# First attention of a two-layer transformer: the value products in two halves between the score rounds, and one of two shifts made by ScalarE and GpSimd

## The chip, the cores and the metric

The kernel runs on one core of a Trainium2 chip. A core has TensorE (matrix products, written PE in the profile, its weight loads PEld), VectorE (DVE), ScalarE (ACT), GpSimd (POOL) and SyncE (SP, which issues most DMAs here). Each engine works through its own instructions in order, and waits for the others by semaphores. Products land in PSUM, which has eight banks of 128 partitions by 512 numbers. The metric is the time of one execution on the device in microseconds (us); smaller is better.

## The reference

The reference takes 64 sequences of 128 tokens with 128 features, all in float32, and applies two layers. Each layer is an attention with 16 heads of 8 features and then a mixture of 8 experts of which 2 are chosen for each token; each part is added to its input, and each starts from a layer norm.

```python
x = x + _L0_xattn_ref(_layernorm(x, axis=-1), fside_BxSxS_0, ctx_1024, ctx_1024, ...)
x = x + _L0_ffn_ref(_layernorm(x, axis=-1), L0_ffn_wqkv, L0_ffn_w1, L0_ffn_w2)
x = x + _L1_xattn_ref(_layernorm(x, axis=-1), ctx_1024, ctx_1024, ...)
x = x + _L1_ffn_ref(_layernorm(x, axis=-1), ...)
```

The first attention is what this case is about. For each sequence, queries come from x. Keys and values come from 128 rows of a side input that are projected, and from 120 rows of a context that are used as they are, so there are 248 keys. Then

```python
attn = jnp.einsum('bhqd,bhkd->bhqk', q, k) * scale
attn = jax.nn.softmax(attn, axis=-1)
out = jnp.einsum('bhqk,bhkd->bhqd', attn, v)
return out.transpose(0, 2, 1, 3).reshape(Bn, Nq, C) @ Wp + bp
```

## The kernel before

The 64 sequences are handled one by one ("batches" in the code), in 16 groups of four (`GB = 4`). `attention` is a pipeline over iterations `it`, one for each batch and five more. In iteration `it` the kernel works on several batches at once:

- **Maxima of batch `it`.** The scores with queries as rows (`max_bank`, L394) are made only for their largest value in each row, which VectorE takes (L414, negated, into `nm`).
- **Shift of batch `it - 1`.** TensorE turns `nm` (two transposes at L459), and VectorE adds the turned maxima to the stored queries `q4` in places where a head's spare feature is multiplied by a one among the keys (L462, once for each half `v` of the heads). So the scores of the second kind come out with the maximum already subtracted.
- **Scores of batch `it - 2`.** They are made again with keys as rows (`score_bank`, L430), and ScalarE takes the exponential into `p` (L438).
- **Values of batch `it - 3`.** `values` (L475) multiplies `p` with the values, which carry a column of ones that gives the sum of each row. There are two halves `v`, with 16 matmuls each, that fill two halves of one bank. ScalarE copies the bank to `ov` (L484, `out1`). TensorE turns it (L491, `out2`), VectorE takes reciprocals of the sums (L495) and scales (L497).
- **Output of batches `it - 4` and `it - 5`.** `out3` turns the result (L504) and ScalarE copies it (L506); `out4` multiplies with the output weights (L511), and `out5` adds to x (L516), followed by statistics for the norms (L109).

The scores are made in four rounds. Each round fills four banks, two with scores for maxima and two with scores for exponentials: TensorE issues the first matmuls of all four, then the second ones, and after that come two maxima on VectorE and two exponentials on ScalarE. All products of the stage draw their bank from one pool of eight (`mtile`); a new one takes the bank that was given back first.

The order is written out by hand: within this stage each engine executes its instructions in the order in which the code emits them. In the first attention an iteration reads:

```python
rounds(0, 1)
on(5, out4); on(1, shift); on(5, out5)
aside.ahead(it); aside.call(it, mtile)
on(3, *vals)
...
prep(it, 0); aside.call(it, mtile)
rounds(2, 3)
on(4, out3); on(3, out2); prep(it, 1)
```

`prep` makes the next group ready, a piece in each half of an iteration. With j the iteration's number modulo 4: at j = 0 the queries (`prep_q`, L292, one matmul and four activations at L301, two in each half, all from one bank); at j = 2 the values of the side input (`prep_v`, L214 and two VectorE additions at L221) in the first half and the keys (`prep_k`, L202 and two activations at L207) in the second; at j = 3 the transposes of x (`prep_x`, L176 and a copy at L177). `context` loads the context's keys (L261) and values (L266) for the next group at j = 2. GpSimd makes the normed x (L167) and its bias (L526).

`aside.call`, twice in an iteration, runs a piece of the first expert layer's router for groups that are done: transposes and logits (L176, L681), choices of the experts by many small VectorE operations, counting (L831), and two indirect DMAs in most iterations, which GpSimd issues (L807). `aside.end` issues zero writes from SP (L1278) that wait for an iteration's L495. After the first attention come the experts' tiles, the second attention (which uses the same function with `first` false), and the second experts.

Of the kernel before, what the change touches and what calls it, by code (L numbers as in the profile page):

```python
# [8 lines left out]
F32 = mybir.dt.float32  # L9
I32 = mybir.dt.int32  # L10
AF = mybir.ActivationFunctionType
ALU = mybir.AluOpType
# [6 lines left out]
GB = 4  # L19
# [25 lines left out]
def transformer_kernel(ctx, tc, a, out):  # L45
# [186 lines left out]
    def attention(layer, w, norm, first, aside):  # L232
# [5 lines left out]
        with ExitStack() as es:  # L238
# [78 lines left out]
            def prep_v(g):  # L317
                values_of(w, src[g], g, n0, mtile())
# [20 lines left out]
            def prep(it, half):  # L339

                g, j = it // GB + 1, it % GB
                if not first:
                    if g == 1:
                        if (j, half) == (0, 0):
                            prep_k(1)
                            prep_v(1)
                        elif (j, half) == (0, 1):
                            prep_x(1)
                        elif j == 1:
                            prep_q(1, half)  # L350
                            if half:
                                prep_heads(1)
                    elif g < NG:
                        pieces = (
                            (), (lambda: prep_k(g), lambda: prep_heads(g)),
                            (lambda: prep_v(g), lambda: prep_x(g)),
                            (lambda: prep_q(g, 0), lambda: prep_q(g, 1)),
                        )[j]
                        if half < len(pieces):
                            pieces[half]()  # L360
                    return
                if half == 0 and it < GB - 1:
                    prep_batch(it + 1)
                if (it, half) == (0, 1):
                    prep_v(0)
                    norm_of(1)
                if (it, half) == (1, 1):
                    biased(0)
                if (it, half) == (2, 1):
                    prep_x(1)  # L370
                if (it, half) == (3, 0):
                    prep_q(1, 0)
                    prep_q(1, 1)
                if (j, half) == (3, 1):
                    if g + 1 < NG:
                        prep_x(g + 1)
                elif g >= NG:
                    return
                elif j == 0 and it:
                    prep_q(g, half)  # L380
                elif (j, half) == (2, 0):
                    prep_v(g)
                elif (j, half) == (2, 1):
                    prep_k(g)


# [68 lines left out]
            def shift(b):  # L455
                g, j = divmod(b, GB)
                pm = mtile()[:, : 2 * S]
                for i in range(2):
                    nc.tensor.transpose(pm[:, i * S : (i + 1) * S], nm[b % 2][:, i, :], ident)  # L459
                for v in range(NV):  # L460
                    q = q4s[g][:, j, 2 * v : 2 * v + 2, :].rearrange("p i q -> p (i q)")
                    nc.vector.scalar_tensor_tensor(  # L462
                        q, pm, smask[:, v : v + 1], q, ALU.mult, ALU.add
                    )

            def values(b, v):
                g, j = divmod(b, GB)
                if v == 0:
                    pavs[b] = mtile()
                pav = pavs[b]  # L470
                p = ps_[b]
                for i in range(2):
                    for c, (_, n) in enumerate(chunks):
                        for ra in range(4):
                            nc.tensor.matmul(  # L475
                                pav[32 * ra : 32 * ra + 32, v * S : (v + 1) * S],
                                lhsT=vs[g % 2][c][:, j, 4 * v + ra, i, :],
                                rhs=p[:n, c, ra, (2 * v + i) * S : (2 * v + i + 1) * S],
                                start=(i == 0 and c == 0), stop=(i == 1 and c == nc_ - 1),
                            )  # L480

            def out1(b):
                ov = rows.tile([128, NV * S], F32, name="ov", tag="ov")
                nc.scalar.copy(ov, pavs.pop(b)[:, : NV * S])  # L484
                ots[b] = ov

            def out2(b):
                ov = ots.pop(b)
# [64 lines left out]
            for it in range(B + 5):  # L553
                def on(back, *steps):
                    b = it - back
                    if 0 <= b < B:
                        for f in steps:
                            f(b)
# [16 lines left out]
                if first:  # L575
# [5 lines left out]
                    on(5, out5)  # L581
                    aside.ahead(it)
                    aside.call(it, mtile)
                    on(3, *vals)
                    if it % GB == 2 and it // GB + 1 < NG:
                        context(it // GB + 1)
                    prep(it, 0)
                    aside.call(it, mtile)
                    rounds(2, 3)
                    on(4, out3)  # L590
                    on(3, out2)
                    prep(it, 1)
                    aside.end(it, work, mtile)
                else:
                    on(3, *vals)
# [970 lines left out]
```

## Time and profile before

| what | us |
|---|---|
| median of three runs | 1524.06 |
| lowest and highest of them | 1517.69, 1524.3 |
| the profiled execution | 1516.1 |
| its span, first to last instruction | 1514.3 |
| TensorE matmuls busy, in the span | 1421.0 |
| VectorE busy | 1102.4 |
| ScalarE busy | 847.6 |
| GpSimd busy | 640.4 |
| maxima, L414, 768 of both attentions | 463.5 |
| shifts, L462, 256 of both attentions | 111.1 |
| copies of the value products, L484, 128 | 48.1 |

The profile is of one execution. A row of a group gives the line, the engine, the operation, what is written and read, its shape and its count; then the busy time and the mean of one in nanoseconds; then the idle time of the engine just before it and who ended most of it. A row of the timeline gives the start, the time, the engine, the line and the operation, with a count where equal ones were merged, and in brackets an idle time before it. A row of the windows gives, for one stretch, the busy time of PE, PEld, DVE, ACT and POOL with their counts, the granted clock, the DMA share and GB/s. Ends of matmuls are modelled and they overlap, so that the busy share of PE is no measure of how near it is to its peak. In float32 each matmul has two records.

### The profile page before, as it was taken

The numbers are of one execution on the slowest core, as the hardware profiler recorded it, in microseconds if no ns is written. First come the engines' busy times: TensorE is split into PE (matmuls) and PEld (weight loads), VectorE is DVE, ScalarE is ACT, GpSimd is POOL, SyncE is SP. The second block draws the span as 40 slices with busy tenths as digits, with TensorE's granted clock in tenths as the row PEclk, the third lists the DMA queues.
The fourth block names the chain that finished last, engine by engine and source line by source line (L and its number), as shares of the span: only waits on it lengthen the run. The fifth ranks groups of instructions, "written<-read, shape, count | busy, mean of one in ns | idle before, by whom it ended". The sixth has DMA issues, their size and how long they took to land.

```text
span 1514.3 us, 42033 instructions
## 1 busy us (share of the span) xinstructions
PE 1421.0 (94%) x16620; PEld 1107.5 (73%) x16620; DVE 1102.4 (73%) x3024; ACT 847.6 (56%) x1740; POOL 640.4 (42%) x1195
## 2 busy tenths in 40 slices
PE   7999999999999999888999999898999999999987
PEld 5777777777777677777888888566666776767665
DVE  6777888888888988455754444687777778787763
ACT  4666666666666666543333333566667566666643
POOL 4123254646465635654001122377546555454210
PEclk9999999999999999999999999899999999999999
DMA  8433333333222221366766667111011111100000
GB/s 201 120 80 80 79 82 96 89 93 94 63 66 60 58 73 40 107 184 202 214 197 199 201 195 205 49 34 34 22 36 29 39 35 32 31 29 23 8 16 22
DMA packets 143719, 133.03 MB, mean 88 GB/s; under 512 B 48546, under 2 KB 126114, under 8 KB 141602
## 3 DMA queue, kind: packets, MB, share of 16 engines
q1 hardware_dynamic: 135330, 113.02, 27.3%
q0 software_dynamic: 8192, 17.32, 3.7%
q8 instruction: 132, 2.16, 0.6%
q14 instruction: 65, 0.53, 0.1%
HBM read 97.32 MB, written 32.97 MB: 86 GB/s over the span
## 4 chain that ended last, share of the span: by engine, by line
PE 69%; DVE 15%; DMA 4%; POOL 4%; ACT 4%; issue 2%; SPq 1%; POOLq 0%; DVEq 0%; ACTq 0%
PE bank L430 11%; PE bank L394 10%; PE bank L475 9%; PE bank L1115 9%; PE bank L1424 4%; PE bank L1445 4%; DVE nm L414 4%; PE bank L1128 3%; DMA q<-xs 2%; PE bank L407 2%; PE bank L214 2%; DVE q L462 2%; PE bank L511 2%; PE bank L681 2%; PE bank L202 2%
## 5 line engine op out<-in xcount | busy, mean ns | idle before, releaser
L414 DVE TENSOR_REDUCE nm<-bank 128x2 f32<-128x496 f32 (+1 forms) x768 | 463.5, 662 | 77.6 <-PE bank L430 61.8
L438 ACT ACTIVATE p<-bank 120x512 f32<-120x512 f32 (+1 forms) x768 | 402.1, 605 | 126.8 <-PE bank L430 123.9
L430 PE MATMUL bank<-q,k 32*120 32x256 f32 (+1 forms) x3072 | 438.1, 399 | 11.4 <-DVE nm L414 5.2
L430 PEld LDWEIGHTS bank<-q,k 32*120 32x120 f32 (+1 forms) x3072 | 293.5, 181 | 56.8 <-DVE nm L414 17.3
L394 PE MATMUL bank<-k,q 32*128 32x248 f32 x2048 | 291.0, 399 | 0.7 <-ACT q L334 0.5
L394 PEld LDWEIGHTS bank<-k,q 32*128 32x128 f32 x2048 | 202.2, 189 | 47.9 <-issue 11.0
L1120 DVE TENSOR_TENSOR p<-p,bank 128x256 f32<-128x256 f32 x213 | 88.0, 420 | 121.0 <-ACT p L1119 120.5
L475 PE MATMUL bank<-p,v 128*32 128x128 f32 (+1 forms) x4096 | 175.6, 275 | 0.2
L407 PE MATMUL bank<-k,qf 32*128 32x480 f32 x512 | 153.8, 602 | 0.8 <-ACT qf L295 0.8
L807 POOL DMA_INDIRECT xs<-xn,at x128 | 129.2, 1009 | 27.9 <-issue 24.3
L1119 ACT ACTIVATE p<-bank 128x256 f32<-128x256 f32 x213 | 81.0, 384 | 98.9 <-PE bank L1115 97.9
L484 ACT COPY ov<-bank 128x256 f32<-128x256 f32 x128 | 48.1, 376 | 143.5 <-PE bank L475 143.4
L475 PEld LDWEIGHTS bank<-p,v 128*32 128x32 f32 (+1 forms) x4096 | 108.8, 109 | 22.8 <-issue 13.7
L1364 POOL DMA_INDIRECT yb<-ys,back x112 | 108.5, 969 | 27.7 <-issue 19.5
L1115 PE MATMUL bank<-q 128*128 128x256 f32 x516 | 118.6, 379 | 1.6 <-ACT q L1106 1.6
L462 DVE SCALAR_TENSOR_TENSOR q<-bank,c_smask,q 128x256 f32<-128x256 f32 x256 | 111.1, 475 | 8.2 <-PE bank L459 7.8
L167 POOL TENSOR_SCALAR xn<-x,mv,rstd 128x128 f32<-128x128 f32 x252 | 110.2, 449 | 7.5 <-issue 1.4
L1115 PEld LDWEIGHTS bank<-q 128*128 128x128 f32 x516 | 94.7, 190 | 13.0 <-ACT q L1106 1.9
L475 PE MATMUL bank<-p,vc 120*32 120x128 f32 x2048 | 103.2, 272 | 0.0
L155 POOL TENSOR_SCALAR rstd<-mv 128x4 f32<-128x4 f32 x32 | 6.3, 198 | 219.9 <-DVE mv L113 123.0
L301 ACT ACTIVATE q<-bank,c_a_bq,c_hmask 128x512 f32<-128x512 f32 x124 | 90.1, 789 | 9.8 <-PE bank L292 9.8
L1157 POOL DMA_INDIRECT kvT<-ys,back x16 | 15.4, 961 | 189.7 <-DMA vc<-xs 114.0
(224 smaller groups left out, 2465.7 us busy)
## 6 DMA issues: line engine op xcount, KB each, us to landing
q<-in_w SPq DMA_DIRECT2D x43, 576.0 KB
vc<-in_w SPq DMA_DIRECT2D x28, 576.0 KB
vc<-in_ctx_v SPq DMA_DIRECT2D x16, 960.0 KB
ys<-zero SPq DMA_DIRECT2D x71, 128.0 KB
k<-in_ctx_k SPq DMA_DIRECT2D x32, 240.0 KB
q<-xs SPq DMA_DIRECT2D x43, 128.0 KB
ys<-q SPq DMA_DIRECT2D x43, 128.0 KB
x<-in_x SPq DMA_DIRECT2D x16, 256.0 KB
```

What stands on the lines that cost most here:

```text
L167: nc.gpsimd.tensor_scalar(xn[:, j, :D], xg[g][:, j, :], self.mv[:, b, 0:1], self.rstd[:, b : b + 1], ALU.add, ALU.mult,)
L301: nc.scalar.activation(q4s[g][:, :, s, :], pq.rearrange("p (b q) -> p b q", b=GB), AF.Identity, bias=w["bq"][:, s : s + 1], scale=hmask[:, ...
L394: nc.tensor.matmul(pa[:, u, :], lhsT=q4s[g][r, j, s, :], rhs=k2[g % 2][r, s // 2, j, :], start=True, stop=True,)
L407: lambda: nc.tensor.matmul(pa, lhsT=qfs[g][r, j, :], rhs=k4s[g][r, :, j, :], start=True, stop=True),
L414: nc.vector.tensor_reduce(nm[b % 2].rearrange("q i (a s) -> q a i s", s=16)[:, 2 * ra + v : 2 * ra + v + len(slots) // 2, :, 0], pa.rearra ...
L430: nc.tensor.matmul(pb[:n, v * 256 : (v + 1) * 256], lhsT=k2[g % 2][r, v, j, k0 : k0 + n], rhs=q4s[g][r, j, 2 * v : 2 * v + 2, :].rearrange ...
L438: nc.scalar.activation(ps_[b][:n, c, ra, :], pb[:n], AF.Exp, scale=SCALE)
L462: nc.vector.scalar_tensor_tensor(q, pm, smask[:, v : v + 1], q, ALU.mult, ALU.add)
L475: nc.tensor.matmul(pav[32 * ra : 32 * ra + 32, v * S : (v + 1) * S], lhsT=vs[g % 2][c][:, j, 4 * v + ra, i, :], rhs=p[:n, c, ra, (2 * v + ...
L807: s = nc.gpsimd.indirect_dma_start(xs, bass.IndirectOffsetOnAxis(at[:, j, k : k + 1], 0), xn, None)
L1115: nc.tensor.matmul(ph[:, u, :], lhsT=w[:, c, u * 128 : (u + 1) * 128], rhs=xT, start=True, stop=True)
L1364: nc.gpsimd.indirect_dma_start(y[:, k, b % 2, :], None, ys, bass.IndirectOffsetOnAxis(back[:, b, k : k + 1], 0),)
```

## The change

The change touches the first attention alone.

- Values are made in two halves that have a bank each. `half_out(b, 0)` stands where all of the values stood, ahead of rounds 2 and 3; `half_out(b, 1)` stands behind them. After each half ScalarE copies 128 columns to `ov`, where one copy of 256 columns was made before.
- Of the two shifts of a batch the second (`v` = 1) is no longer made by VectorE. ScalarE copies the turned maxima, scaled by the mask, to a tile `sh` (which shares its two buffers with `ov`), and GpSimd adds `sh` to the queries.
- `prep_v` for the next group moves behind rounds 2 and 3 of the same iteration, with `context`, and `prep_k` takes its place ahead of them.
- `out2` moves behind `prep(it, 1)`.

```diff
@@ prep @@
                 elif (j, half) == (2, 0):
-                    prep_v(g)
-                elif (j, half) == (2, 1):
                     prep_k(g)
@@ shift @@
                 for v in range(NV):
                     q = q4s[g][:, j, 2 * v : 2 * v + 2, :].rearrange("p i q -> p (i q)")
+                    if first and v:
+
+                        sh = rows.tile([128, 2 * S], F32, name="sh", tag="ov")
+                        nc.scalar.activation(sh, pm, AF.Copy, scale=smask[:, v : v + 1])
+                        nc.gpsimd.tensor_tensor(q, q, sh, ALU.add)
+                        continue
                     nc.vector.scalar_tensor_tensor(
                         q, pm, smask[:, v : v + 1], q, ALU.mult, ALU.add
                     )
@@ values @@
-                if v == 0:
+                if v == 0 or first:
                     pavs[b] = mtile()
@@ after out1 @@
+            def half_out(b, v):
+
+                values(b, v)
+                if v == 0:
+                    ots[b] = rows.tile([128, NV * S], F32, name="ov", tag="ov")
+                cols = slice(v * S, (v + 1) * S)
+                nc.scalar.copy(ots[b][:, cols], pavs.pop(b)[:, cols])
@@ the loop over iterations, first attention @@
                     aside.call(it, mtile)
-                    on(3, *vals)
-                    if it % GB == 2 and it // GB + 1 < NG:
-                        context(it // GB + 1)
+                    on(3, lambda b: half_out(b, 0))
                     prep(it, 0)
                     aside.call(it, mtile)
                     rounds(2, 3)
+                    on(3, lambda b: half_out(b, 1))
+                    if it % GB == 2 and it // GB + 1 < NG:
+                        context(it // GB + 1)
+                        prep_v(it // GB + 1)
                     on(4, out3)
+                    prep(it, 1)
                     on(3, out2)
-                    prep(it, 1)
                     aside.end(it, work, mtile)
```

## The prediction

> **What bounds the kernel now.** I read the page's engine row first, then the windows, then the timeline of each engine over four iterations, because the change lies in the first attention alone (about 15 to 625 us).
>
> ```profile
> PE 1421.0 (94%) x16620; PEld 1107.5 (73%) x16620; DVE 1102.4 (73%) x3024; ACT 847.6 (56%) x1740; POOL 640.4 (42%) x1195
> L484 ACT COPY ov<-bank 128x256 f32<-128x256 f32 x128 | 48.1, 376 | 143.5 <-PE bank L475 143.4
> L462 DVE SCALAR_TENSOR_TENSOR q<-bank,c_smask,q 128x256 f32<-128x256 f32 x256 | 111.1, 475 | 8.2 <-PE bank L459 7.8
> ```
>
> ```profile
> 200.00:400.00 200.00, 197.39 (x3037) 149.63 (x3033) 171.22 (x432) 129.61 (x262) 116.10 (x259) 1.00 0.32 85
> ```
>
> In that window (columns PE, PEld, DVE, ACT, POOL, clock, DMA) TensorE looks full and VectorE is 86% busy. But matmuls overlap, so the share hides stalls. The pace shows them: with every bank free, a pair of rounds (32 matmul records) takes 1.91 us to issue. That is what the second rounds from 323.69 to 325.60 take; from 316.76 to 319.71 the first rounds take 2.95:
>
> ```profile
> 315.23 0.47 PE L430 MATMUL bank<-q,k 32*120 32x256 f32 x1 [0.31 <-DVE nm L414]
> ...
> 316.28 0.33 PE L504 MATMUL bank<-ident,o 128*128 128x128 f32 x1
> ...
> 318.66 0.48 PE L430 MATMUL bank<-q,k 32*128 32x256 f32 x1
> ...
> 319.71 0.49 PE L511 MATMUL bank<-c_a_wo,oT 128*128 128x128 f32 x2
> ```
>
> ```profile
> 317.13 1.47 ACT L301 ACTIVATE q<-bank,c_a_bq,c_hmask 128x512 f32<-128x512 f32 x2
> ```
>
> At 315.23 and 318.66 TensorE resumes when a PSUM bank comes back: the first from VectorE's maximum, the second from ScalarE's query activations. So the bound is TensorE plus the return of eight banks. Iterations begin at 316.76, 326.14, 336.04, 345.08, 354.46, 363.85, 373.97, 382.26 and 391.65: 74.89 us for eight, 9.36 each. Call them phases 1, 2, 3, 0, 1', 2', 3', 0' (iteration number modulo 4; the router's work differs between the two groups). Over 1.91 us, the first rounds lose 1.04, 0.86, 0.75, 0.5 in phases 1, 2, 3, 0; the second rounds lose 1.0 in phase 0 alone, where the query bank leaves only seven. The reason is visible: 1.90 us of values plus output work stand ahead of the second rounds, but only 0.54 us of transposes ahead of the first.
>
> **The change, part by part**, in us from the first matmul of an iteration. From the timelines: the first maximum starts 1.13 after its round pair, four take 2.34; the first exponential 1.18, four take 1.92; out4 with the shift's transposes is 0.63 of TensorE; values 1.90, so a half 0.95; a bank is used again 0.07 after its reader; a second round needs its last bank at +0.90, and lasts 1.05 from there.
>
> *Removed from VectorE:* one of two shifts, 0.39 back to back, so 64 x 0.39 = 25 us of busy time. It shortens the time from the first rounds' last maximum (3.47) to the router's operations.
>
> *Added to ScalarE:* the scaled copy of 128x256, which no row shows. Nearest is the copy-out of that size, 0.376; the 128x512 query activation with scale and bias is 0.79. Bounds 0.37 to 0.79; I take 0.40. Two copies of 128x128 replace one of 128x256: 2 x 0.29 (the row of oT's copy) - 0.376 = +0.2. ScalarE goes from 6.0 to 6.6 us of 9.4, so its busy time isn't the price; its order is.
>
> Here a rule speaks against the change. The Trainium skill, "PSUM — Partial Sum Buffer", section on bank collisions: two engines may not touch the same bank and quadrant at once, reads against reads included. The shift's bank now has two readers, and in the built program the scaled copy indeed waits for VectorE's shift. Without the rule it would run at 3.10, when the exponentials end; with it at 3.47 + 0.39 + 0.07 = 3.93, done at 4.33. Queued behind it are half 0's copy-out, then phase 1's xnT copy, phase 3's router exponential, phases 0 and 2's query or key activations, and the second rounds' exponentials. In phases 0 and 2 nothing is lost (query or key matmul ends at 4.55 anyway). In phase 1 the logits matmul waits for xnT: 4.33 + 0.60 + 0.07 = 5.00 against 4.69, +0.31. In 3' half 0's copy-out ends at 5.22, and the last bank of the second rounds is 0.88 late.
>
> *Added to GpSimd:* an add of 128x256; its row, `x<-x,yb` of the same size, has 0.734. Its result is due at the next iteration's first score matmuls, some 5 us after 4.33, so it is hidden; were the cover gone it would cost 0.73 x 64 = 47 us. Behind it wait the router's operations and indirect DMAs; only phase 2' feels it: products 1.07 on GpSimd, for which a VectorE reduction waits until 6.27 (the maxima behind it slip 1.3). A second rule, "SBUF — State Buffer", section "SBUF: two separate sides": a GpSimd operation that reads SBUF and a VectorE one with two SBUF inputs exclude each other for the whole instruction. The rows don't agree:
>
> ```profile
> 322.32 0.22 DVE L719 TENSOR_TENSOR eq<-eq,order 128x64 f32<-128x64 f32 x1
> ```
>
> ```profile
> 322.25 0.21 POOL L138 TENSOR_TENSOR mv<-st 128x4 f32<-128x4 f32 x1 [2.49 <-DVE st L109]
> 322.41 0.20 POOL L139 TENSOR_TENSOR d<-st 128x4 f32<-128x4 f32 x1
> ```
>
> VectorE's product of two SBUF tiles runs through both in its usual 0.22. I take nothing; by the rule up to 0.73 an iteration, 47 us.
>
> *Moved on TensorE:* half of the values, 0.95, from ahead of the second rounds to behind them. Gains: the first rounds find their banks free (1.91 in phases 0, 2, 3). Losses: the second rounds start 0.95 earlier relative to VectorE's work; and out2 now needs the second half's copy-out. That wait is new: half 1 ends at E, its copy runs E + 0.13 to E + 0.40 (or behind the exponentials), the second transpose at 0.07 more, the next rounds 0.2 later: 0.67 after E, where out3 and out2 took 0.48. Behind it stand all next rounds. Value projection (1.09, phase 2) and xnT's transposes (0.56, phase 3) fill it.
>
> *Moved with it:* prep_k's matmul (1.06) and two activations (1.34) from behind the second rounds to ahead of them in phase 2, prep_v the other way with its two VectorE adds (0.67 back to back). SP's values DMA of the context waits for half 1 instead; behind it stand only zero writes and the next load, and it is needed five iterations later: nothing. Its two key DMAs don't wait for the values: nothing.
>
> **The sum.** Phase 1: query activations of phase 0 still hold a bank until 1.53; first rounds end 2.58; out4, shift, xn transposes (0.53) to 3.74, half 0 to 4.69, logits 5.00 to 6.00, second rounds to 7.91, half 1 to 8.86, exponentials end 9.10, copy 9.37, next rounds 9.64 (was 9.38).
> Phase 2: 1.91 + 0.63 + 0.95 + 1.06 = 4.55; the last bank waits for the key activations (4.65 + 1.53), rounds end 7.23, half 1, prep_v, out3, out2: 9.75 (was 9.90).
> Phase 3: the router's counting matmul waits for its VectorE operand, which was 5.02 into the iteration and is now ready at 4.77; TensorE now comes at 3.51, waits to 4.94: 9.40 (was 9.04).
> Phase 0: second rounds start at 4.55, their last bank needs the first new maximum, VectorE is at the router until 5.95: bank at 6.60, rounds end 7.65; 9.27 (was 9.38).
> By the same steps 1' 9.64 (9.39), 2' 10.12 (10.12), 3' 8.33 (8.29), 0' 9.54 (9.39).
> Together 75.69 against 74.89: +0.8 for eight, x 8 = +6.4 us. The profiled execution took 1516.1 (span 1514.3 and 1.8 around it), so it would take 1522.5; the median shown is 1524.06, 8 above it, and the forecast stands on that: 1530. In short, the removed stalls (about 2.5 us per four iterations) come back as later banks in the second rounds, a logits wait, a counting wait and the copy-out.
>
> **Rivals.** *The stalls really go (1494):* the first rounds' stalls fall by 0.5, 0.5, 0.86, 0.7 in phases 0 to 3, and neither the second rounds nor out2 take it back; less 0.19 x 2 of longer tails that is about 2.2 per four, or 35 us over 64. For it: VectorE's 86%, relieved by 0.39 an iteration. Against it: VectorE works 2.1 to 2.8 us between the two round pairs even so, and TensorE then arrives 0.95 earlier. Chance 0.22.
> *ScalarE's queue becomes the chain (1556, slower):* the place is the scaled copy behind VectorE's shift. My sum has 0.3 us or less to spare between it and the query and key activations. If the first rounds' maxima end later than about 3.5, or the copy takes the upper bound's 0.79, each further 0.1 moves activations, exponentials and half 1's copy by 0.1; at 0.4 that is 64 x 0.4 = 26 us more. For it: the ordering is certain. Against it: VectorE's maxima ended 3.47 to 3.8 after the start already. Chance 0.31.
> *Nothing moves:* DMA and GpSimd hide all; it falls in the likeliest case.
>
> **Numbers.** The likeliest case, 1530 with its own range 1518 to 1544 (0.1 to 0.2 us an iteration of error in the steps), has 0.47: 0.03 of it faster, 0.22 the same, 0.22 slower. The rivals give 0.20 faster and 0.02 same, and 0.29 slower and 0.02 same. A difference under 0.5% (7.6 us; the three runs spread 0.43%) can't be told from none. Faster 0.23, same 0.26, slower 0.51. The range takes in both rivals' values and a little of the added bounds: 1498 to 1562.
>
> **What would show it.** First rounds near 1.91 us in phases 0, 2, 3; the scaled copy starting right behind VectorE's shift; TensorE's wait ahead of out2's second transpose in phases 0 and 1; the counting matmul waiting for VectorE; the second rounds of phase 2 near 2.7; the add done 3 us or more before its reader. An iteration under 9.0 us on average, or over 9.7, makes the forecast wrong.

## The result, and the profile after

The changed kernel took 1535.65 us (median of seven executions), the kernel before 1521.57 on the same chip: a ratio of 1.0092, with a 95% interval of 1.0074 to 1.011, or 14 us more. One of the seven took 6383 us and is left out of the ratio. The profiled execution took 1536.61, its span 1534.8 (before: 1516.1 and 1514.3).

The page's engine row, and from it and the list of all groups the rows of the lines that were changed (busy us, mean ns of one, then the idle time before it):

```profile
PE 1413.3 (92%) x16620; PEld 1094.3 (71%) x16620; DVE 1092.1 (71%) x2960; ACT 880.0 (57%) x1868; POOL 688.7 (45%) x1259
L466 DVE SCALAR_TENSOR_TENSOR q<-bank,c_smask,q 128x256 f32<-128x256 f32 x192 | 86.0, 475 | 8.7 <-PE bank L457 8.5
L464 POOL TENSOR_TENSOR q<-q,sh 128x256 f32<-128x256 f32 x64 | 47.9, 749 | 253.7 <-ACT sh L463 240.7 <-DVE eq L732 7.8 <-DVE te_i_a L948 5.1
L497 ACT COPY ov<-bank 128x128 f32<-128x128 f32 x128 | 34.4, 269 | 20.4 <-PE bank L479 20.4
L463 ACT ACTIVATE sh<-bank,c_smask 128x256 f32<-128x256 f32 x64 | 30.4, 475 | 56.4 <-DVE q L466 56.4
```

GpSimd is 48.3 us busier, ScalarE 32.4. VectorE loses only 10.3, although its shifts' row fell by 25.1 (111.1 to 86.0): other operations of it got longer, above all a 128x64 product (5.3 us over 38), a 128x8 operation with a scalar (2.7 over 19), a scan (2.6 over 8) and a cast (1.0 over 16). The last row's idle time, 56.4 us, is the scaled copy waiting for VectorE's shift of the same bank. The window between 200 and 400 us (PE, PEld, DVE, ACT, POOL, clock, DMA share, GB/s):

```profile
200.00:400.00 200.00, 189.10 (x2979) 141.25 (x2983) 164.90 (x400) 138.67 (x301) 127.47 (x268) 1.00 0.32 85
```

TensorE's busy time in it fell from 197.39 to 189.10 at an unchanged clock: it waits more. Where it waits is read from TensorE's timeline, cut into four stretches for each phase: first rounds, what stands between ("middle"), second rounds, and what stands behind them up to the next iteration ("tail"). Here are the stretches between 240 and 480 us, where the pattern of eight iterations repeats within 0.03 us:

| phase | before: first, middle, second, tail | period | after: first, middle, second, tail | period | forecast |
|---|---|---|---|---|---|
| 1 | 2.96, 3.97, 1.91, 0.54 | 9.38 | 2.38, 3.67, 1.99, 1.73 | 9.77 | 9.64 |
| 2 | 2.77, 3.62, 2.03, 1.48 | 9.90 | 1.91, 2.71, 2.66, 2.43 | 9.71 | 9.75 |
| 3 | 2.66, 3.28, 1.91, 1.19 | 9.04 | 2.20, 3.29, 1.91, 1.93 | 9.33 | 9.40 |
| 0 | 2.41, 3.59, 2.92, 0.48 | 9.39 | 1.93, 2.71, 3.38, 1.73 | 9.75 | 9.27 |
| 1' | 2.96, 3.98, 1.91, 0.54 | 9.39 | 2.38, 3.67, 1.91, 1.81 | 9.76 | 9.64 |
| 2' | 2.77, 3.62, 2.09, 1.64 | 10.12 | 1.91, 2.71, 3.08, 2.43 | 10.14 | 10.12 |
| 3' | 2.66, 2.53, 1.91, 1.19 | 8.29 | 2.20, 1.65, 2.54, 1.93 | 8.32 | 8.33 |
| 0' | 2.40, 3.59, 2.92, 0.48 | 9.39 | 1.91, 2.71, 3.34, 1.73 | 9.69 | 9.54 |

Eight iterations take 76.49 us instead of 74.89. That is +1.6, or 12.8 us if all 64 iterations were like these. They are not quite: over the 58 full iterations of the two traces (539.2 and 552.5 us) the difference is 13.3 us. The first eight are 1.6 faster, each of the next four eights is 1.6 slower, and the eight from 437 us on are 4.2 slower. There one phase 0 takes 13.31 us instead of 9.75 (10.28 in the kernel before), with TensorE's granted clock (third number from the right) at a half:

```profile
512.00:519.00 7.00, 6.58 (x64) 4.71 (x67) 2.75 (x6) 3.08 (x6) 4.26 (x9) 0.51 0.06 20
```

In the kernel before, the clock is 1.00 in these 7 us. Whether the change brings the half clock about is not shown.

The tail contains half 1 of the values (0.95) now, and the middle lacks it. So the first rounds are shorter everywhere, as the removed stalls said; the second rounds are longer in both phases 2 and 0 and in 3', and the tail is longer by more than half 1 in both phases 0 and 1 (0.48 to 1.73, 0.54 to 1.73 or 1.81).

The wait that sets phase 0, and the scaled copy, in the timelines of TensorE and ScalarE after (phase 0 begins at 350.88):

```profile
357.85 0.47 PE L428 MATMUL bank<-q,k 32*120 32x256 f32 x1 [0.77 <-DVE nm L412]
```

```profile
354.92 0.47 ACT L463 ACTIVATE sh<-bank,c_smask 128x256 f32<-128x256 f32 x1 [0.80 <-DVE q L466]
355.29 0.26 ACT L497 COPY ov<-bank 128x128 f32<-128x128 f32 x1
...
360.05 0.27 ACT L497 COPY ov<-bank 128x128 f32<-128x128 f32 x1 [0.33 <-PE bank L479]
```

TensorE's last bank of the second rounds comes 6.97 after the phase began, from VectorE's maximum; 6.60 was forecast. Why VectorE is late is in its own timeline. First VectorE in two places, then GpSimd in the same two:

```profile
336.65 0.63 DVE L733 TENSOR_TENSOR eq<-eq,order 128x64 f32<-128x64 f32 x1
...
355.69 0.70 DVE L856 TENSOR_TENSOR_SCAN sums<-flat,zero 128x64 f32<-128x64 f32 x1
```

```profile
336.43 0.78 POOL L464 TENSOR_TENSOR q<-q,sh 128x256 f32<-128x256 f32 x1 [0.32 <-ACT sh L463]
...
355.48 0.76 POOL L464 TENSOR_TENSOR q<-q,sh 128x256 f32<-128x256 f32 x1 [4.33 <-ACT sh L463]
```

The product of two SBUF tiles is the operation that the prediction showed at 0.22 beside small GpSimd operations; beside the 128x256 add it takes 0.63. The scan takes 0.70, and 0.29 in the kernel before:

```profile
350.43 0.29 DVE L842 TENSOR_TENSOR_SCAN sums<-flat,zero 128x64 f32<-128x64 f32 x1
```

Both end just after the add does (337.28 against 337.21, 356.39 against 356.24).

### The profile page after: what moved, and what is told of

Read it like the earlier page. It is cut to its first block, busy times and chain, and to the rows that moved or that the text cites. A ratio compares the mean times of both kernels' runs of the same rounds, so it can differ in the third digit from the quotient of the medians.

```text
span 1534.8 us, 42093 instructions
## 1 busy us (share of the span) xinstructions
PE 1413.3 (92%) x16620; PEld 1094.3 (71%) x16620; DVE 1092.1 (71%) x2960; ACT 880.0 (57%) x1868; POOL 688.7 (45%) x1259
## 3 DMA queue, kind: packets, MB, share of 16 engines
q8 instruction: 131, 2.15, 0.6%
## 4 chain that ended last, share of the span: by engine, by line
PE 58%; DVE 22%; ACT 7%; POOL 5%; DMA 5%; issue 3%; SPq 0%; POOLq 0%; ACTq 0%; DVEq 0%
PE bank L1129 9%; DVE nm L412 8%; PE bank L428 7%; PE bank L479 7%; PE bank L392 7%; PE bank L1438 4%; PE bank L1459 4%; PE bank L1142 3%; ACT p L436 3%; DVE q L466 3%; DMA q<-xs 2%; PE bank L405 2%; PE bank L214 2%; DMA vc<-xs 2%; PE bank L503 2%
## 5 line engine op out<-in xcount | busy, mean ns | idle before, releaser
L428 PE MATMUL bank<-q,k 32*120 32x256 f32 (+1 forms) x3072 | 419.6, 396 | 17.3 <-DVE nm L412 10.6
L392 PE MATMUL bank<-k,q 32*128 32x248 f32 x2048 | 268.2, 397 | 0.5 <-ACT q L334 0.5
L392 PEld LDWEIGHTS bank<-k,q 32*128 32x128 f32 x2048 | 189.8, 191 | 39.0 <-DVE st L109 15.2
L479 PE MATMUL bank<-p,v 128*32 128x128 f32 (+1 forms) x4096 | 179.2, 280 | 6.5 <-DVE nm L412 5.6
L464 POOL TENSOR_TENSOR q<-q,sh 128x256 f32<-128x256 f32 x64 | 47.9, 749 | 253.7 <-ACT sh L463 240.7
L479 PEld LDWEIGHTS bank<-p,v 128*32 128x32 f32 (+1 forms) x4096 | 104.9, 110 | 51.8 <-DVE nm L412 27.2
L167 POOL TENSOR_SCALAR xn<-x,mv,rstd 128x128 f32<-128x128 f32 x252 | 111.1, 453 | 8.6 <-issue 2.5
L466 DVE SCALAR_TENSOR_TENSOR q<-bank,c_smask,q 128x256 f32<-128x256 f32 x192 | 86.0, 475 | 8.7 <-PE bank L457 8.5
```

The costliest lines, as they stand in the source:

```text
L167: nc.gpsimd.tensor_scalar(xn[:, j, :D], xg[g][:, j, :], self.mv[:, b, 0:1], self.rstd[:, b : b + 1], ALU.add, ALU.mult,)
L392: nc.tensor.matmul(pa[:, u, :], lhsT=q4s[g][r, j, s, :], rhs=k2[g % 2][r, s // 2, j, :], start=True, stop=True,)
L428: nc.tensor.matmul(pb[:n, v * 256 : (v + 1) * 256], lhsT=k2[g % 2][r, v, j, k0 : k0 + n], rhs=q4s[g][r, j, 2 * v : 2 * v + 2, :].rearrange ...
L466: nc.vector.scalar_tensor_tensor(q, pm, smask[:, v : v + 1], q, ALU.mult, ALU.add)
L479: nc.tensor.matmul(pav[32 * ra : 32 * ra + 32, v * S : (v + 1) * S], lhsT=vs[g % 2][c][:, j, 4 * v + ra, i, :], rhs=p[:n, c, ra, (2 * v + ...
```

## The experiments

The experiments ran on other chips than the measurement above, and a kernel's time differs between these by up to 3.6% (the kernel before: 1518 to 1573 us), so each is set against the kernel before on its own chip, by the ratio. Part of what the chips do differently turned out to matter here: how much an indirect DMA of the router disturbs the engines around it.

A second measure goes round that. Iterations 13 to 20 (the eight that end at about 200 us) come before the first indirect DMA, and there the changed kernel takes the same time on the three chips on which it was profiled: 76.47 us on the first, 76.48 and 76.47 on two others. So the traces of all versions can be compared there. A later eight (29 to 36, from about 280 us) shows what the time with the indirect DMAs adds. Each value is from one execution:

| version | iterations 13 to 20 | against the kernel before, times 8 | iterations 29 to 36 |
|---|---|---|---|
| kernel before, first chip | 74.89 | | 74.90 |
| changed kernel, first chip | 76.47 | +12.6 | 76.48 |
| changed kernel again | 76.48 | +12.7 | 81.93 |
| split alone | 76.07 | +9.4 | 78.45 |
| shift alone | 74.75 | -1.1 | 75.88 |
| scaled copy first | 74.99 | +0.8 | 78.59 |
| add twice | 77.50 | +20.9 | 81.62 |
| without the add | 75.60 | +5.7 | 82.44 |
| output's transposes later | 75.81 | +7.4 | 79.52 |
| router's second piece later | 72.88 | -16.1 | 76.29 |
| that, and the add later | 72.04 | -22.8 | 86.01 |

The sections below call the first column the undisturbed iterations. It leaves out what the router does only later: the router's second piece moved, without indirect DMAs, takes 72.90 in the first column and 73.23 in the last.

### The split alone, and the shift alone

The split alone keeps both shifts on VectorE:

```diff
 for v in range(NV):
     q = ...
-    if first and v:
-        sh = rows.tile(...)
-        nc.scalar.activation(sh, pm, AF.Copy, scale=smask[:, v : v + 1])
-        nc.gpsimd.tensor_tensor(q, q, sh, ALU.add)
-        continue
     nc.vector.scalar_tensor_tensor(...)
```

> Both shifts on VectorE again, the rest of the change kept. Theory (the moved half of the values costs, because VectorE's work between the round pairs loses its cover): nearly the whole slowdown stays, 1530 to 1540 against 1521 before, since VectorE gets 0.39 us per iteration more while ScalarE's wait for it is gone. Rival (the hand-over of the shift to ScalarE and GpSimd costs): most of the 14 us is gone, 1521 to 1527.

The shift alone puts these five lines into the kernel before, with all values in one piece ahead of the second rounds.

> The kernel before with the second shift by ScalarE and GpSimd alone. Theory: 1.9 us of value products cover both the 0.39 us that VectorE saves and the later scaled copy, so nothing moves, 1516 to 1526. Rival (the hand-over costs): 1529 to 1535. If VectorE's busy time were the bound: 64 x 0.39 = 25 us less, about 1497.

Measured: the split alone 1.0094 (1.0062 to 1.0126), the shift alone 1.0005 (0.9986 to 1.0024). VectorE's relief and the new hand-over over ScalarE and GpSimd, taken alone, change nothing that can be measured; in the kernel before, both have cover. That holds for GpSimd's add too: with the shift alone it lengthens the same VectorE operations as in the changed kernel (the eight scans take 4.9 us together, 2.35 in the kernel before), and it costs nothing. The split alone makes the kernel slower, by some 15 us on this chip. The whole change costs 35 us there (below), so the split and the shift do not simply add up: in the split kernel the shift by ScalarE and GpSimd costs about 20 us more. In the undisturbed iterations it is only 0.4 us in eight, 3 us in all. Most of the rest goes with the indirect DMAs: with the split alone 22 copies start late for 22 us in all, in the changed kernel 26 for 33 us. In the profile of the split alone the logits' wait of phase 1 is shorter than in the changed kernel (middle 3.09, not 3.67), since no scaled copy stands ahead of the xnT copy, and the second rounds take most of it back (2.44, not 1.99). In phase 0', with both shifts on VectorE, TensorE waits 1.07 us for VectorE's maximum:

```profile
315.59 0.47 PE L428 MATMUL bank<-q,k 32*120 32x256 f32 x1 [1.07 <-DVE nm L412]
```

### The scaled copy ahead of VectorE's shift

```diff
-for v in range(NV):
+for v in ((1, 0) if first else (0, 1)):
```

> The changed kernel with the order of the two shifts turned: ScalarE's scaled copy first, so it doesn't wait for VectorE's shift on the same bank. Theory: the copy starts about 0.8 us earlier, which gives back about 0.3 us in phase 1 (the logits wait for xnT) and 0.4 in every second phase 3, and GpSimd's add ends before VectorE's router operations start, which gives back about 0.4 in phase 0: 8 to 14 us less than the changed kernel, about 1524. Rival (the order on the bank is not on the path): within 3 us of 1535.

Measured 1.0084 (1.0058 to 1.0109). The changed kernel itself on that chip, run later, gave 1.0228 (below), so this order is some 22 us better there, more than expected. Part of that is the indirect DMAs again (18 late copies of 17 us, not 26 of 33). In the undisturbed iterations it is 1.5 us in eight, or 12 us over 64, which is what was expected. The scaled copy now runs as soon as the exponentials are done, and what stood behind it comes earlier: in 2' the products on GpSimd (second rounds 2.66, not 3.09), in 1' the logits (middle 3.09, not 3.67), in 3' half 0's copy (second rounds 2.21, not 2.54), in 0 VectorE's router (3.18, not 3.39). VectorE's shift is later for it, and some comes back: phase 1's middle is 3.09 (3.67) but its second rounds are 2.33 (1.99), in phase 3 the counting matmul makes the middle 3.47 (3.29), and in 0' the second rounds are 3.46 (3.34).

### GpSimd's add twice

```diff
 nc.gpsimd.tensor_tensor(q, q, sh, ALU.add)
+again = rows.tile([128, 2 * S], F32, name="again", tag="again", bufs=1)
+nc.gpsimd.tensor_tensor(again, sh, sh, ALU.add)
```

> The changed kernel with a second GpSimd addition of the same size behind the first (sh + sh into a tile that nobody reads). Theory (GpSimd's add and VectorE's operations between SBUF tiles exclude each other, as the 0.70 us scan and the 0.69 us tensor_scalar in the changed kernel's trace suggest): up to 0.75 us more of VectorE's router time where it is on the path, 8 to 20 us slower than the changed kernel, and again VectorE operations that last until the end of an addition. Rival (the two engines don't hinder each other): 0 to 3 us slower.

Measured 1.027 (1.0238 to 1.0302). Against the changed kernel's 1.0228 (1.0199 to 1.0257) on that chip this is about 7 us, with intervals that overlap. The undisturbed iterations show it more surely: 1.0 us more in eight, or 8 us over 64, with 0.58 of it in phase 2' (10.73 against 10.14, where the products wait behind both adds) and 0.30 in phase 0 (10.05 against 9.75). The second add is 39.7 us of GpSimd's time, so most of it is hidden. The scan of phase 0 takes 702 ns here, no more than with one add: it is the first add that meets it. The second add meets the operation behind the scan, a 128x8 one of two SBUF tiles that takes 0.17 otherwise. It ends with the add, and TensorE's wait for the first new maximum grows from 0.77 to 1.07:

```profile
284.14 0.42 DVE L864 TENSOR_TENSOR start<-filled,sums 128x8 f32<-128x8 f32 x1
```

```profile
283.92 0.61 POOL L466 TENSOR_TENSOR again<-sh 128x256 f32<-128x256 f32 x1
```

### The changed kernel again, and without the add

The changed kernel as it is:

> The changed kernel itself, on the chip that the following kernels use, so that each can be set against it. If the price of the change belongs to the program and not to one chip, the ratio to the kernel before is again 1.007 to 1.011, and the stretches of each phase come out as in the first profile (phase 0 near 9.7 us, phase 1 near 9.8). If the chip has a part in it, ratio and phases differ.

The same without `nc.gpsimd.tensor_tensor(q, q, sh, ALU.add)`:

> Left out: GpSimd's add of the scaled copy to the queries, so half of the heads are not shifted and the output differs. ScalarE's copy stays. Theory A, GpSimd's add holds up VectorE operations that run beside it (0.17 us ones grew to 0.69): VectorE's operations go back to their usual lengths, phase 0 loses about 0.4 us, phases 1 and 1' about 0.1 each: 0.8 to 1.6 us for eight iterations, 6 to 13 us less than the changed kernel. Theory B, the add is hidden and the second rounds' later banks are the whole price: within 3 us of the changed kernel.

Measured: again 1.0228 (1.0199 to 1.0257), so the change cost 35 us on this chip and not 14; without the add 1.0168 (1.0144 to 1.0193), 8.6 us less. For the add, the mechanism is shown: the eight scans are back at 293 ns, TensorE's wait in phase 0 is half,

```profile
L855 DVE TENSOR_TENSOR_SCAN sums<-flat,zero 128x64 f32<-128x64 f32 x8 | 2.3, 293 | 0.3
```

```profile
282.01 0.47 PE L428 MATMUL bank<-q,k 32*120 32x256 f32 x1 [0.39 <-DVE nm L412]
```

and phase 0 takes 9.37 instead of 9.75; phase 0' takes 9.64 instead of 9.69. That is 0.43 us in eight iterations, 3.4 in all. In the undisturbed iterations the add has a second price of the same size: without it phase 2' takes 9.71 and not 10.14, because the products no longer stand behind it on GpSimd (the prediction had this wait in its sum). Together that is 0.87 in eight, or 7 of the 8.6 us. In the later iterations of this run neither can be read off the total, because on this chip something else moves by more.

What that is, the repeated kernel tells. Its stretches are those of the first chip within 0.03 us up to 204 us. From then on, which is when the router's indirect DMAs have begun, the tail of phase 1 grows from 1.73 to 3.0 and that of phase 3 from 1.93 to 3.36. Set side by side instruction by instruction, nearly every step by which the second execution falls behind begins at ScalarE's copy of half 1. GpSimd's and ScalarE's timelines around the same place of the pattern, a phase 1', on the first chip and then on this one:

```profile
369.22 1.11 POOL L821 DMA_INDIRECT xs<-xn,at  x1 [0.17 <-DVE nm L412]
...
369.78 0.30 ACT L497 COPY ov<-bank 128x128 f32<-128x128 f32 x1
```

```profile
293.52 1.11 POOL L821 DMA_INDIRECT xs<-xn,at  x1 [0.17 <-DVE nm L412]
...
294.98 0.97 POOL L821 DMA_INDIRECT xs<-xn,at  x1 [0.16 <-issue]
295.56 0.27 ACT L497 COPY ov<-bank 128x128 f32<-128x128 f32 x1 [1.32 <-PE bank L503]
```

The values' last matmul ends at 293.99, and ScalarE is free from 294.24, yet the copy starts at 295.56: 2.04 after the first of two indirect DMAs started. Of 128 copies 26 start more than 0.35 us late in this way, 33 us together; on the first chip none does. TensorE then waits for the copy to turn its second half.

### The output's transposes an iteration later, and the router's second piece later

```diff
 on(5, out5)
+on(4, out2)
 ...
 prep(it, 1)
-on(3, out2)
```

> The output's transposes (out2) move from behind the second half of the values to the next iteration, behind the shift, so that nothing on TensorE waits for ScalarE's copy of half 1. Theory A, that hand-over is a price of the split in phases 0, 1, 3: the stretch behind the second rounds falls from 1.73 to 1.81 us to about 1.2 (half 1 0.95 and out3 0.24), the two transposes cost 0.27 in the middle instead, net 0.25 to 0.35 us an iteration: 16 to 22 us less than the changed kernel, below the kernel before. Theory B, VectorE sets the second rounds and only gets two more operations (0.7 us) ahead of the router's: what the tail gains, the middle and the second rounds lose, within 5 us of the changed kernel or slower.

```diff
 prep(it, 0)
-aside.call(it, mtile)
 rounds(2, 3)
 on(3, lambda b: half_out(b, 1))
+aside.call(it, mtile)
```

> The second of the router's two pieces of work in an iteration moves from ahead of the second rounds to behind half 1 of the values. Theory A: its matmuls then stand where TensorE waits for ScalarE's copy, and the counting matmul's wait for VectorE (phase 3) and the logits' wait for xnT (phase 1) are gone from the middle: 2.5 to 3.5 us for eight iterations, 20 to 28 us less than the changed kernel, 5 to 14 less than the kernel before. Theory B: TensorE only comes earlier to second rounds whose banks VectorE and ScalarE return no sooner, so that the middle shrinks and the second rounds grow by as much: within 6 us of the changed kernel.

Measured: 1.0111 (1.0088 to 1.0134) and 0.997 (0.9959 to 0.9981). Against the changed kernel on this chip that is 17 and 39 us less. With the transposes moved, the tails of phases 0 and 1 are 1.28, so nothing on TensorE waits for half 1's copy any more; the late copies are still there (24, 29 us) and no longer count in phase 1. But the kernel does not get below the one before. The middle takes the two transposes, and phase 1's first rounds take 2.83 instead of 2.38. So the number is theory A's, but not for its reason: in the undisturbed iterations only 0.67 us in eight are gained, 5 us over 64, as theory B said. The other 12 us appear only with the indirect DMAs.

The second piece moved gave more than theory A asked for, against the changed kernel (39 us, expected 20 to 28; 29 by the undisturbed iterations), and it is the one version with the full computation that is faster than both kernels. Against the kernel before it gained less (4 us, expected 5 to 14). Phase 1's middle is 2.09 (3.67), phase 3's 1.65 (3.29): the logits' and the counting matmul's waits are gone. The second rounds give back less, 2.15 (1.99) and 2.63 (1.91). Tails of 2.6 to 3.4 remain in phases 2 and 3, with 23 late copies of 31 us.

### Plain DMAs in place of the indirect ones

```diff
-s = nc.gpsimd.indirect_dma_start(
-    xs, bass.IndirectOffsetOnAxis(at[:, j, k : k + 1], 0), xn, None)
+n = E * CAP + (2 * j + k) * S
+s = nc.sync.dma_start(xs[n : n + S], xn)
 ...
-for dst, src in ((x, xs[bass.ds(r, TT), :D]), ...):
+n0 = E * CAP + (t % (GA * GB)) * TT
+for dst, src in ((x, xs[n0 : n0 + TT, :D]), ...):
```

> The kernel before, with its indirect DMAs (GpSimd writes each batch's rows where the router sends them) replaced by plain DMAs of the same rows that the sync queue issues, to fixed rows; the experts then read those fixed rows, so the output is not the reference's. It is the base for the next kernel. If the indirect DMAs cost the kernel before time on this chip, it falls by 10 to 40 us; if they are hidden there, by under 5 us.

> The changed kernel with the same replacement (output not the reference's). Theory A: of the changed kernel's 35 us on this chip, some 20 come from ScalarE's copy of half 1, which starts only 2.0 us after the first of two indirect DMAs that GpSimd issues just then, and the remaining 14 are the split's own. Then no copy of half 1 starts late, the tails of phases 1 and 3 are 1.8 and 1.9 us again, and this kernel stands 10 to 18 us above the one before with plain DMAs. Theory B: the late copies have another cause (ScalarE's order, or the chip): tails of 2.7 to 3.4 us remain, and the distance stays 30 to 40 us.

Measured on one chip: the kernel before with plain DMAs 1532.45 us, 0.9772 (0.975 to 0.9794); the changed kernel with plain DMAs 1546.26, 0.9856 (0.9836 to 0.9876). So the kernel before is 36 us faster on this chip without its indirect DMAs. Most of that lies behind the first attention: from its last full iteration to the end this trace takes 935 us, and those with indirect DMAs on these chips 955 to 968. There the experts' reads were changed too, so that part isn't the indirect DMAs' alone. Without them the distance between the two kernels is 13.8 us: that of the first chip, where they cost nothing of this kind. Every stretch of the changed kernel is back within 0.02 us of the table above, no copy is late (the version of the next section ran on this same chip with indirect DMAs, and had 15), and ScalarE's waits are those of the first chip (us in total, times, longest):

```profile
ACT p L436 <- PE bank L428: 48.9, 39, 2.1
ACT sh L463 <- DVE q L466: 25.5, 32, 0.8
ACT ov L497 <- PE bank L479: 8.0, 20, 0.7
```

With the indirect DMAs, in the repeated kernel, over the same 300 us:

```profile
ACT ov L497 <- PE bank L503: 18.2, 14, 1.5
ACT ov L497 <- PE bank L479: 7.4, 13, 1.4
```

Theory A holds: the change's own price is 14 us, and the other 20 or so come from the indirect DMAs that now meet half 1's copy. (The 35 us are from one chip and the 13.8 from another, on which the changed kernel with indirect DMAs wasn't run; the kernel before takes 1573 and 1569 us on them.)

### GpSimd's add behind the router's first piece

To the second piece moved, this adds:

```diff
-nc.gpsimd.tensor_tensor(q, q, sh, ALU.add)
+adds.append((q, sh))
 ...
 aside.call(it, mtile)
+for q, sh in adds:
+    nc.gpsimd.tensor_tensor(q, q, sh, ALU.add)
+adds.clear()
 on(3, lambda b: half_out(b, 0))
```

> The changed kernel with the router's second piece behind half 1 of the values, and GpSimd's add of the scaled copy behind the router's first piece instead of ahead of it. Theory A: GpSimd then issues the indirect DMAs 0.8 us earlier, so half 1's copy waits less for them, and the router's operations on VectorE that ran beside the add no longer do: 5 to 20 us less than with the second piece moved alone, 10 to 25 us below the kernel before. Theory B: the add only meets other VectorE operations, and the router's first piece made GpSimd late anyway: within 5 us of it.

Measured 1.0255 (1.023 to 1.0281): 45 us worse than the version that it starts from, where 5 to 20 better was expected. Up to the first indirect DMA it is better, as expected: the undisturbed iterations take 72.04 and not 72.88, which would be 7 us over 64, and no score matmul waits for the add between 100 and 204 us. From then on the waits between 100 and 500 us show what is new:

```profile
POOL mv L138 <- DVE st L109: 80.8, 19, 6.9
...
PEld bank L428 <- POOL q L597: 23.7, 11, 2.8
POOL q L597 <- ACT sh L463: 21.5, 9, 9.0
PE bank L428 <- POOL q L597: 19.4, 11, 2.4
```

GpSimd's timeline, and the score matmul that wants the result:

```profile
293.10 1.11 POOL L824 DMA_INDIRECT xs<-xn,at  x1 [0.18 <-issue]
...
294.56 0.97 POOL L824 DMA_INDIRECT xs<-xn,at  x1 [0.16 <-DVE rs L507]
295.55 0.73 POOL L597 TENSOR_TENSOR q<-q,sh 128x256 f32<-128x256 f32 x1
```

```profile
296.34 0.48 PE L428 MATMUL bank<-q,k 32*128 32x256 f32 x1 [1.18 <-POOL q L597]
```

Ahead of the add now stand the router's small operations, which wait for VectorE up to 6.9 us, and then two indirect DMAs, 2.8 us with what goes with them. The small operations wait as long before 204 us, and the add is still in time; with the indirect DMAs it is not. The score matmuls wait for it, and the first rounds of a phase 1' take 4.8 us instead of 2.4. The 45 us can't be divided: TensorE's granted clock, too, is only 0.96 from 50 to 600 us in this trace, and 1.00 in that of the version that it starts from. I had looked at what the add delays, and not at what it is queued behind.

### The later second piece with plain DMAs

> The changed kernel with the router's second piece behind half 1 of the values, and with the plain DMAs to fixed rows in place of the indirect ones (output not the reference's). Theory A: moving that piece takes back the waits of the middle in phases 1 and 3 and gives TensorE work while half 1 is copied; on this chip half of that gain was hidden by copies that started late (31 us of them in the run with indirect DMAs). Without them it stands 10 to 22 us below the kernel before with plain DMAs (1532), at 1510 to 1522. Theory B: the tails of 2.4 to 3.3 us that the moved piece showed are the piece's own matmuls and VectorE's time, not the indirect DMAs: within 6 us of 1532.

Measured 1491.99 us against 1518.05 of the kernel before (with its indirect DMAs) on a chip of the first kind: 0.9822 (0.98 to 0.9844). By its own stretches eight iterations take 73.2 us (phases 0 to 3: 9.35, 9.00, 9.71, 8.85; then 9.27, 9.12, 9.71, 8.22), 1.7 below the kernel before and 3.3 below the changed one: 13 and 26 us over 64. The tails of phase 3 are 2.37 here, and 3.3 with indirect DMAs; those of phase 1 are 2.39 both ways, so these are the moved piece's own matmuls. Theory A is right on what the piece's place is worth. The other 13 us by which this run is below the kernel before lie behind the first attention (904 us from its last full iteration on, and 918 in the kernel before), where the plain DMAs are new too. In the first attention the kernel before takes 74.89 in eight iterations with either kind of DMA.

## Why the prediction was right, and where it was off

**The sum.** Forecast +6.4 us for the change, 1530 in all; measured +14 and 1535.65, inside the likeliest case's own range, but the forecast price is less than half of the measured one. It was slower, and for the reason named: "the removed stalls come back as later banks in the second rounds, a logits wait, a counting wait and the copy-out".

**Phases 2, 3, 2', 3'.** 9.71, 9.33, 10.14 and 8.32 against 9.75, 9.40, 10.12 and 8.33. The bank from the key activations (phase 2), the counting matmul (3), the products on GpSimd (2') and half 0's copy (3') are where the steps put them. The first rounds of both phases 3 took 2.20, though, and not the 1.91 that the forecast had for phase 3. The add is done 3.0 to 4.8 us before its reader from iteration 12 on, as the prediction asked.

**Phase 0, the term that was mis-sized.** 9.75 against 9.27, +0.48 of the total miss of 0.8 in eight iterations; 0.37 of it is the bank and 0.11 the tail. The step is "VectorE is at the router until 5.95", and under it "I take nothing" for the rule of the Trainium skill, "SBUF — State Buffer", section "SBUF: two separate sides": a VectorE operation with two SBUF inputs and a GpSimd one that reads SBUF shut each other out. I weighed the rule against the one meeting that the trace before shows, small GpSimd operations of 128x4, beside which the product kept its 0.22. The add isn't of that size. Beside it the same product takes 0.63 and the scan 0.70, and the first new maximum starts at 6.24. The rule holds here. VectorE loses some 12 us to it in all, but what it costs the kernel is neither that nor the 47 us of every add: it is 0.4 us in the one phase of eight where the operation it meets sets TensorE's next bank, 3 us over the whole. The run without the add gives 0.38 of phase 0 back, and the one with two adds takes 0.30 more. For this term neither the row that I chose nor the rule's full price was right; the size of the operation and what waits for it decide.

**The tails.** "0.67 after E" for out2 is 0.78 in phases 0 and 0' (tails of 1.73, less half 1's 0.95) and 0.86 in 1': half 1's copy starts 0.20 after E where 0.13 was forecast, and all behind it is that much later. With 0.05 to 0.1 in the second rounds of phase 1 and the middle of 1', which begin 6.05 after the phase and not 6.00, this is the rest of the miss, some 0.1 in each of four phases.

**The scaled copy.** It starts 4.04 after the phase begins (forecast 3.93) and hands on at 4.41 (4.33): VectorE's read of the same bank comes first. 0.40 was taken for its time; alone it is 0.475, and the next copy starts 0.37 after it.

**The rivals.** "The stalls really go": the first rounds fell by 0.48, 0.58, 0.86 and 0.46 in phases 0 to 3, what this rival asked for in phases 0 to 2 (it had 0.7 for phase 3). It fell because the second condition did, that the second rounds take nothing back: TensorE came earlier to banks that were not there. (Its 1494 is not what its own terms give: 35 us below the 1524.06 on which the forecast stood is 1489.) "ScalarE's queue becomes the chain": its place is real, since the copy ahead of the shift takes back about 12 us by the undisturbed iterations; the Trainium skill's rule that two engines may not read the same quadrant of one bank at once ("PSUM — Partial Sum Buffer", on bank collisions) agrees with the 0.80 that the copy sits idle before VectorE's shift lets it go, and this price comes from it. But it stays at what the sum had for it and doesn't grow to that rival's 26 us: the copy starts 0.11 later than forecast and not 0.4. What did make the kernel as slow as that rival's number on the other chips (+35 us) was none of the cases named: half 1's copy meeting the indirect DMAs.

**The base.** The forecast stood on 1524.06; the kernel before has 1521.57 in seven executions, so 2.5 us of the error were made up there. That the total came out within 6 us is in that part luck: the change alone was missed by almost 8.

## What to carry to other kernels

When work is moved to take stalls out of one stage, follow TensorE to the next stage and ask which bank it finds there, and who gives it back at what time: here eight iterations saved 4.8 us in their first rounds and still ended 1.6 us longer. A cut that brings a new hand-over (half 1, its copy, its transpose) needs other TensorE work between, and here the router's second piece was at hand: moved behind half 1 it made the kernel faster than both. An operation that is given to GpSimd is to be priced by what it is queued behind (two indirect DMAs made the late add miss its reader), and by the VectorE operations that run beside it.

## What the runs showed of the hardware

- A GpSimd add of 128x256 from SBUF holds VectorE operations on SBUF up to the end of the add: a product of 128x64 goes from 0.22 to 0.63 us, a scan of 128x64 from 0.29 to 0.70. A second add behind the first holds the next operation (128x8, from 0.17 to 0.42). An operation on one small SBUF tile with a scalar is held, too:

```profile
346.25 0.69 DVE L762 TENSOR_SCALAR s<-e 128x8 f32<-128x8 f32 x1
```

This one took 0.17 before.

- On two chips, and not on the first, engines that wait for TensorE are held while GpSimd issues indirect DMAs. Most of the late copies in the repeated changed kernel start 2.02 to 2.08 us after the first of two such DMAs started, or 1.56 to 1.62 after the second. The same is seen with VectorE and ScalarE at once, in the same trace:

```profile
341.85 1.04 POOL L821 DMA_INDIRECT xs<-xn,at  x1 [0.16 <-issue]
...
342.98 0.59 PE L428 MATMUL bank<-q,k 32*120 32x256 f32 x2
...
343.50 0.43 PE L479 MATMUL bank<-p,v 128*32 128x128 f32 x8
...
343.87 1.26 DVE L412 TENSOR_REDUCE nm<-bank 128x2 f32<-128x496 f32 x2 [0.47 <-PE bank L428]
343.92 0.60 ACT L436 ACTIVATE p<-bank 120x512 f32<-120x512 f32 x1 [0.45 <-PE bank L428]
```

Both go on 2.02 and 2.07 after the DMA started, while TensorE itself issues the values on time. That points to TensorE's signals arriving late, and not to an engine that is held; it is argued from these rows, and no run separates it. That the indirect DMAs are the cause is shown by the two runs on such a chip without them (no late copy in the changed kernel). These runs changed both the kind of the DMA and the engine that issues it, SyncE and not GpSimd, and no run tells which of the two matters. Why some chips do it is open.
